# Gate r, value and hawk output as seven products of half matrices, with tokens on partitions, in a fused Hawk and RWKV block

## The chip, the cores and the metric

The kernel runs on one core of one Trainium2 chip. The metric is the device time of one execution in microseconds (us); the median of three runs of the kernel before is 644.53 us. The engines are TensorE (PE in the profile, its weight loads PEld), VectorE (DVE), ScalarE (ACT), GpSimd (POOL) and SyncE (SP), which here only issues DMAs.

## The reference

The input x has 8 sequences of 1024 tokens and 256 channels, all in fp32. The output is the sum of x and two branches that read the same normalized input.

```python
xn = _layernorm(x, axis=-1)
x = x + _L0_attn_ref(xn, ...) + _L0_ffn_ref(xn, ...)

# attn ("hawk"): 256 channels, 384 hidden
gate = einsum('bsd,hd->bsh', x, Wg)
u    = einsum('bsd,hd->bsh', x, Wi)
y    = conv1d(u, conv_w, 4 taps, causal, one per channel) + conv_b
ig   = sigmoid(einsum('bsh,gh->bsg', y, lru_Wi) + lru_bi)
rg   = sigmoid(einsum('bsh,gh->bsg', y, lru_Wg) + lru_bg)
alpha = exp(-8 * softplus(lam) * rg)
beta  = sqrt(1 - alpha**2 + 1e-6)
h     = scan over tokens: h[t] = alpha[t] * h[t-1] + beta*ig*y
out   = einsum('bsh,dh->bsd', gelu(gate) * h, Wo)

# ffn ("rwkv" channel mix): 256 channels
xr = mu_r * x + (1 - mu_r) * x_prev      # x_prev: x shifted by one token
xk = mu_k * x + (1 - mu_k) * x_prev
r  = sigmoid(einsum('btc,dc->btd', xr, W_r))
out = r * einsum('btc,dc->btd', square(relu(xk @ W_k.T)), W_v)
```

## The kernel before

The eight sequences are worked off one after the other. The input of a sequence is loaded with tokens on partitions (`xs`, two buffers), normalized there (`stats`, `deviation`, `inverse`, `normalize`), turned on TensorE by 16 transposes of 128 columns (`transposes`, L541) and kept with channels on partitions in `xnT`. From there come the branches:

- family u (gate and u, six blocks of 128 rows), family k (the key) and family l (the two lru gates, three chunks of 128 channels deep) run with channels on partitions: a weight block of 128x128 is loaded, and 512 tokens stream past it (`product`, L305). The output lies in one PSUM bank of 128x512.
- gate r (`r_product`), value (`v_product`) and the hawk output (`o_product`) run with tokens on partitions (`by_token`, L594): 128 tokens are the loaded operand, and the 256 columns of the weight stream past. r and value have two chunks of 128 channels, the hawk output three. A bank takes two tiles of 128 tokens.

Every fp32 matmul of the program appears in the trace as two passes, each with its own weight load.

**Seven products.** The families u, k and l do a 2x2 product of blocks (two row blocks, two channel chunks, two halves of 512 tokens) with seven products where eight would be needed, in the manner of Strassen and Winograd. The class `Group` holds one such set. Its token sums T0 to T3 are differences of halves of the input, made on GpSimd (`token_sum`, L302); its weight sums S0 to S3 are made once (`weight_sums`). Step 1 makes A and C, and ScalarE copies A into a new bank B (`seed`, L360) and C into SBUF (`five`, L365). Step 2 adds to A, which can then be evicted, and to B. Then VectorE's `fork_c` (L368) writes B + five into C, and step 3 adds to B (its first product) and to C. `fork_d` (L376) writes B + five to the place of the fourth quarter, and step 4 adds to B. A third chunk, as in family l, is added by plain products, and then the fourth quarter has a bank D and a step 5; without one, `late` finishes the fourth quarter from SBUF. An eviction of a quarter is `evict`; after it the bank is free.

**Order.** All instructions of all engines are put in one list of steps with a time, and the list is sorted. TensorE's products have times that follow one another (`pe`, `clock`, `now()`): one unit is one product of 512 columns, two passes. Everything else is put in by `at`, whose default time is relative to TensorE's clock and is replaced by an entry of the table `PLACES` where there is one (times in the same units from the start of the sequence; one table for the first, one for the middle, one for the last sequence). Each engine does its instructions in the order that comes out; semaphores see to the data. So a place fixes an order within an engine's queue, not a moment. In a middle sequence TensorE's order in before has 91 units: u, k, the end of the last sequence's l, then r, value, the hawk output of the sequence before (`outs`), the own l, and among that the transposes of the next sequence (`tp`).

**Around the change.** `add_x` (L629) adds x once more, by an accumulating DMA from GpSimd's queue into `sides` (two buffers, tokens on partitions), where r's tanh and then the value product are kept. `add_hawk` (L639) adds the hawk output to it on VectorE and issues the output's DMA on SP. `conv_rest` (L658) is the convolution's second to fourth tap, three each for three chunks; `mix` (L580) makes xk and xr; `recur` (L690) is the scan; `decay`, `decay_square`, `decay_rest`, `beta`, `gated_input`, `scaled_input`, `gated_state` surround it. `decay_rate` (L249 to L261) makes a constant of three columns. `key_home` is where the activated key lies: in `ysum`, in the last sequence in the first buffer of x.

Of the kernel before, what the change touches and what calls it, by code (L numbers as in the profile page):

```python
# [10 lines left out]
ALU = mybir.AluOpType  # L11
# [23 lines left out]
        "u0_0 evict 0 0": 2.36, "u0_0 evict 1 0": 3.48, "u0_0 evict 0 1": 6.36, "u1 seed": 9.36,  # L35
        "u0_0 evict 1 1": 10.05, "u1 five": 10.73, "stats 0 8": 10.89, "u2 seed": 11.41,
        "conv_first 1": 12.09, "u1 evict A 0 0": 13.51, "u2 five": 14.19, "k seed": 15.36,
        "u1 fork_c": 16.16, "stats 0 1": 16.96, "k five": 17.27, "stats 1 1": 17.69,
        "conv_first 0": 17.95, "u2 fork_c": 18.36, "deviation": 19.3, "u1 fork_d": 19.36,
        "u2 evict A 0 0": 21.18, "inverse 0 8": 21.66, "u1 evict C 0 1": 21.86, "k fork_c": 22.36,  # L40
        "k evict A 0 0": 22.54, "conv_first 2": 23.22, "u2 fork_d": 23.36, "conv_rest 0 1": 24.17,
        "u2 evict C 0 1": 24.57, "normalize 0 1": 25.25, "stats 2 1": 25.66, "u1 evict B 1 0": 25.95,
        "k fork_d": 26.36, "normalize 1 1": 26.64, "conv_rest 0 2": 27.17, "k late": 27.34,
        "normalize 2 1": 28.02, "conv_rest 1 1": 28.66, "u2 evict B 1 0": 28.73, "k evict B 1 0": 29.41,
        "conv_rest 0 3": 30.16, "k evict C 0 1": 31.19, "conv_rest 2 1": 31.65, "r_tanh 0": 32.97,
        "conv_rest 1 2": 33.13, "r_tanh 2": 33.66, "normalize 3 1": 34.34, "conv_rest 2 2": 34.63,
        "normalize 4 1": 35.03, "r_tanh 4": 35.74, "conv_rest 1 3": 36.12, "normalize 5 1": 36.42,
        "normalize 6 1": 37.11, "conv_rest 2 3": 37.61, "r_tanh 6": 37.81, "normalize 7 1": 38.5,
        "stats 3 1": 39.09, "u1 late": 39.19, "value 0": 39.75, "u2 late": 39.87, "stats 4 1": 40.55,
        "y_sum 0": 40.86, "stats 5 1": 41.27, "value 2": 41.93, "y_sum 1": 42.09, "stats 6 1": 42.73,  # L50
        "value 4": 43.38, "stats 7 1": 44.19, "y_sum 2": 44.86, "value 6": 45.36, "y_sum 3": 46.02,
        "l0 seed": 46.3, "add_x": 46.98, "l0 five": 47.15, "l0 evict A 0 0": 49.36, "l0 fork_c": 50.36,
        "l1 seed": 51.36, "put_transposed 0 0": 52.86, "put_transposed 1 0": 53.44, "l1 five": 54.01,
        "put_transposed 0 1": 54.69, "l0 fork_d": 55.36, "put_transposed 1 1": 55.38, "x_sum 0": 55.54,
        "mix_before k 0": 56.06, "x_sum 2": 56.7, "mix_before k 1": 57.29, "mix k 0": 57.87,
        "l0 evict C 0 1": 58.51, "mix_before r 0": 59.31, "mix k 1": 59.36, "l0 evict B 1 0": 60.54,
        "mix r 0": 60.86, "l1 evict A 0 0": 61.36, "mix_before r 1": 62.16, "x_sum 1": 62.36,
        "l1 fork_c": 62.36, "l0 evict D 1 1": 63.39, "k_sum 0": 63.52, "l2 seed": 64.36,
        "mix r 1": 64.68, "l2 five": 65.36, "decay 0": 66.05, "k_sum 1": 66.18, "l1 fork_d": 66.36,
        "x_sum 3": 67.35, "decay 1": 67.39, "k_sum 2": 68.51, "l1 evict C 0 1": 68.73,  # L60
        "decay_square 0": 69.53, "k_sum 3": 69.67, "l2 evict A 0 0": 70.64, "l2 fork_c": 71.36,
        "decay 2": 71.44, "decay_rest 0": 72.17, "decay_square 1": 72.78, "l1 evict B 1 0": 73.89,
        "decay_rest 1": 74.06, "l1 evict D 1 1": 74.69, "l2 fork_d": 75.36, "decay_square 2": 75.49,
        "decay_rest 2": 77.59, "l2 evict C 0 1": 86.13
    },
    "middle": {
        "gated_input 0": -0.83, "beta 0": 0.33, "stats 0 1": 0.59, "stats 1 1": 1.32, "u0 seed": 1.56,
        "scaled_input 0": 1.98, "beta 1": 2.24, "stats 2 1": 3.4, "u0 five": 3.47, "recur 0 L": 4.06,
        "beta 2": 4.15, "u0 evict A 0 0": 5.38, "stats 3 1": 5.52, "recur 0 R": 6.18,
        "l2 evict B 1 0": 7.56, "u0 fork_c": 7.63, "gated_state 0": 8.44, "l2 evict D 1 1": 9.16,  # L70
        "gated_input 1": 9.86, "u1 seed": 9.96, "k seed": 10.64, "gated_input 2": 11.29,
        "u1 five": 11.32, "k five": 12.01, "u0 fork_d": 12.71, "scaled_input 1": 13.52,
        "deviation": 14.19, "u0 evict C 0 1": 14.57, "scaled_input 2": 14.94, "u1 evict A 0 0": 15.25,
        "conv_first 0": 15.93, "u1 fork_c": 16.37, "recur 1 L": 17.17, "k evict A 0 0": 17.28,
        "u0 evict B 1 0": 18.36, "k fork_c": 18.63, "conv_first 1": 19.12, "recur 2 L": 19.43,
        "u2 seed": 20.46, "recur 1 R": 20.89, "u2 five": 21.14, "u1 fork_d": 22.34,
        "u1 evict C 0 1": 22.36, "conv_first 2": 23.12, "recur 2 R": 23.14, "k fork_d": 24.6,
# [70 lines left out]
def kernel(  # L148
# [182 lines left out]
    class Group:  # L331
# [11 lines left out]
        def step(self, n):  # L343
# [34 lines left out]
            def late():  # L378
                self.out(1, 1, "sbuf")
# [673 lines left out]
```

## Time and profile before

| what | us |
|---|---|
| median of 3 runs | 644.53 (644.47 to 645.62) |
| the profiled execution, its own time | 645.16 |
| its span in the profile | 643.2 |
| TensorE busy in the span | 637.7 (99%) |
| VectorE / ScalarE / GpSimd busy | 469.5 / 458.9 / 186.4 |
| the same in a middle sequence, 314.90 to 393.25 (78.35) | 57.74 / 57.41 / 20.82 |

The granted clock of TensorE was 1.0 in the profiled execution. The durations of matmuls in the profile are from the start of a pass to its modelled end, and passes overlap; so the spacing of starts, which the chain gives as a stretch's length for so many passes, says what a pass costs TensorE. In the rows of groups the columns are line, engine, operation, output and inputs with their shape, count, busy time in us, mean ns of one, and the idle time before. The table of stretches has the stretch and its length, then busy us and count for PE, PEld, DVE, ACT and POOL, the granted clock, the DMA share and GB/s.

### The profile page before, as it was taken

The page shows a single profiled execution, that of the slowest core. Times are in us where ns is not written, and L with a number is a line of the kernel's source. Part 1 is how long each engine was busy: PE and PEld are TensorE (multiplying, and loading weights), DVE is VectorE, ACT ScalarE, POOL GpSimd, SP SyncE. Part 2 cuts the span into 40 slices and gives each one's busy share as a digit, 9 for nine tenths or more (in the row PEclk, how much of TensorE's full clock was granted, in tenths as well). Part 3 has the DMA queues.
Part 4 walks back from the last instruction along what each step waited for, and adds up shares of the span by engine and source line. Part 5 has one row for each costly group of instructions (what it writes and reads, how often), then busy time and mean ns, then how long its engine had stood idle before and what let it go on. Part 6 is the DMA issues. An engine that isn't in the chain of part 4 may idle for free.

```text
span 643.2 us, 5932 instructions
## 1 busy us (share of the span) xinstructions
PE 637.7 (99%) x2032; PEld 372.6 (58%) x2032; DVE 469.5 (73%) x602; ACT 458.9 (71%) x646; POOL 186.4 (29%) x131
## 2 busy tenths in 40 slices
PE   9999999999999999999999999999999999999997
PEld 4475446864468544775447754486544865456466
DVE  4896799656995669847699377992779827798395
ACT  3895998368873888639885398845988269883870
POOL 4926600443004620047101380022800328104000
PEclk9999999999999999999999999999999999999999
DMA  9205100260004400052000520006000060000412
GB/s 317 77 1 92 40 0 1 41 155 2 0 1 67 130 0 1 1 102 94 0 0 2 114 83 0 0 1 114 18 0 0 2 114 17 1 0 1 65 34 98
DMA packets 27549, 28.70 MB, mean 45 GB/s; under 512 B 1152, under 2 KB 27008, under 8 KB 27520
## 3 DMA queue, kind: packets, MB, share of 16 engines
q1 hardware_dynamic: 18784, 19.53, 9.4%
q0 software_dynamic: 8320, 8.39, 8.7%
q10 hardware_dynamic: 416, 0.41, 0.2%
q8 instruction: 16, 0.26, 0.2%
q14 instruction: 13, 0.11, 0.1%
HBM read 19.94 MB, written 8.39 MB: 44 GB/s over the span
## 4 chain that ended last, share of the span: by engine, by line
PE 98%; DVE 1%; ACT 0%; issue 0%; DVEq 0%
PE bank L305 65%; PE bank L594 30%; PE bank L541 2%; PE bank L776 1%; DVE st L514 0%; ACT x L536 0%; ACT u L445 0%; DVE xnT L558 0%; ACT xnT L560 0%; DVE mv L516 0%; DVE side L639 0%; DVE mv L527 0%; DVEq L1048 0%; ACT std L519 0%; DVE five L752 0%
## 5 line engine op out<-in xcount | busy, mean ns | idle before, releaser
L305 PE MATMUL bank<-y,w_l 128*128 128x512 f32 x288 | 137.8, 592 | 0.0
L302 POOL TENSOR_TENSOR ysum<-y 128x512 f32<-128x512 f32 x16 | 24.2, 1513 | 298.1 <-PE bank L594 277.6
L305 PEld LDWEIGHTS bank<-y,w_l 128*128 128x128 f32 x288 | 54.6, 190 | 62.6 <-issue 61.2
L658 DVE SCALAR_TENSOR_TENSOR y<-u,par,y 128x1024 f32<-128x1024 f32 x72 | 88.8, 1288 | 0.0
L594 PE MATMUL bank<-w_o,g 128*128 128x256 f32 x384 | 86.1, 379 | 0.0
L594 PEld LDWEIGHTS bank<-w_o,g 128*128 128x128 f32 x384 | 73.0, 190 | 15.9 <-issue 6.7
L305 PE MATMUL bank<-ysum,sum_l 128*128 128x512 f32 x144 | 72.3, 593 | 0.0
L305 PE MATMUL bank<-xsum,sum_u 128*128 128x512 f32 x138 | 69.1, 592 | 0.0
L536 ACT ACTIVATE x<-x,mv,std 128x256 f32<-128x256 f32 x60 | 31.6, 591 | 52.0 <-DVE mv L527 52.0
L368 DVE TENSOR_TENSOR bank<-bank,five 128x512 f32<-128x512 f32 x55 | 38.0, 691 | 38.5 <-PE bank L305 38.5
L594 PE MATMUL bank<-w_r,xr 128*128 128x256 f32 x256 | 58.8, 379 | 0.0
L594 PEld LDWEIGHTS bank<-w_r,xr 128*128 128x128 f32 x256 | 48.6, 190 | 16.0 <-issue 8.9
L457 ACT ACTIVATE tr<-bank,half_b 128x512 f32<-128x512 f32 x48 | 32.3, 687 | 31.5 <-PE bank L305 31.5
L305 PE MATMUL bank<-xnT,w_u 128*128 128x512 f32 x108 | 54.1, 593 | 0.7 <-ACT xnT L560 0.7
L639 DVE TENSOR_TENSOR side<-side,bank 128x512 f32<-128x512 f32 (+1 forms) x36 | 22.1, 624 | 41.8 <-PE bank L594 41.8
L376 DVE TENSOR_TENSOR bank<-bank,five 128x512 f32<-128x512 f32 x24 | 16.8, 699 | 44.8 <-PE bank L305 44.8
L594 PE MATMUL bank<-w_v,ysum 128*128 128x256 f32 x224 | 49.5, 379 | 0.0
L360 ACT COPY bank<-bank 128x512 f32<-128x512 f32 x55 | 31.7, 577 | 22.9 <-PE bank L305 22.2
L594 PEld LDWEIGHTS bank<-w_v,ysum 128*128 128x128 f32 x224 | 42.6, 190 | 5.8
L302 POOL TENSOR_TENSOR xsum<-xnT 128x512 f32<-128x512 f32 x16 | 21.1, 1331 | 84.4 <-ACT xnT L560 84.4
L305 PEld LDWEIGHTS bank<-ysum,sum_l 128*128 128x128 f32 x144 | 26.7, 190 | 31.0 <-issue 26.5
L305 PEld LDWEIGHTS bank<-xsum,sum_u 128*128 128x128 f32 x138 | 26.1, 189 | 30.1 <-issue 28.3
(113 smaller groups left out, 1147.4 us busy)
## 6 DMA issues: line engine op xcount, KB each, us to landing
side<-in_x_dram POOLq DMA_DIRECT2D x8, 1024.0 KB, 11.0
x<-in_x_dram SPq DMA_DIRECT2D x7, 1024.0 KB, 5.5
out_dram<-side SPq DMA_DIRECT2D x28, 256.0 KB, 3.6
x<-in_x_dram SPq DMA_DIRECT2D x4, 256.0 KB, 4.3
out_dram<-side SPq DMA_DIRECT2D x8, 128.0 KB, 1.7
w_l<-in_lru_wg_dram SPq DMA_DIRECT2D x1, 576.0 KB, 6.0
w_l<-in_lru_wi_dram SPq DMA_DIRECT2D x1, 576.0 KB, 7.0
w_u<-in_w_i_dram ACTq DMA_DIRECT2D x1, 384.0 KB, 3.9
```

Of the source, the lines that this page charges most:

```text
L302: nc.gpsimd.tensor_tensor(dst[o], a, b, ALU.subtract)
L305: nc.tensor.matmul(banks[b], lhsT, rhs, start=start, stop=True, skip_group_check=True)
L360: nc.scalar.copy(banks[bank["B"]], banks[bank["A"]])
L368: nc.vector.tensor_tensor(banks[bank["C"]], banks[bank["B"]], self.five, ALU.add)
L376: nc.vector.tensor_tensor(d, banks[bank["B"]], self.five, ALU.add)
L457: nc.scalar.activation(dst[:, m, HALVES[h]], src, AF.Tanh, bias=half_b[:, b + m : b + m + 1], scale=0.5)
L536: nc.scalar.activation(xa, xa, AF.Identity, bias=m, scale=r)
L541: nc.tensor.matmul(banks[b][:, t * P : (t + 1) * P], xs[s % 2][:, 4 * h + t, c * P : (c + 1) * P], ident, is_transpose=True, start=(t == 0 ...
L594: nc.tensor.matmul(banks[b][:, j * D : (j + 1) * D], lhs[:, c, (t + j) * P : (t + j + 1) * P], weights[w][:, c, :], start=(j == 0 and c == 0),
L639: nc.vector.tensor_tensor(o, o, two_tiles(b)[:, j : j + n, :], ALU.add)
L658: nc.vector.scalar_tensor_tensor(y[:, m, :], u[:, m, k : k + S], column(COL_CONV_W + k * HC + m), y[:, m, :], ALU.mult, ALU.add,)
L776: nc.tensor.matmul(banks[b], warm[:, 0:P], warm, start=True, stop=True)
```

## The change

Gate r, value and the hawk output become `Group`s of seven products too, with tokens on partitions. A product of such a group takes a half of 512 tokens, one chunk of channels and 128 of the 256 output columns, and runs as four matmuls, one for each tile of 128 tokens, each with 128 columns of weight (`product_by_token`). A quarter of the result lies in a bank as four tiles of 128 tokens by 128 columns and goes to a quadrant of `sides`. r is a group in all sequences, value in all but the first, the hawk output (with a third chunk in plain products) for all sequences but the last two; those keep `by_token`. In a middle sequence TensorE's list has 88 units instead of 91.

The token sums of the new groups need room: `sums_for` gives r three buffers of its own and half of xr, value those of x (`xsum`), k the buffer in `sides` of the same sequence, the hawk output `tr`. x has one buffer `xt` instead of two; sequence s + 2 is loaded after the transposes of s + 1, at time `now() + 1`, and all its statistics are in the places from 73 on. The constants of `decay_rate` are steps of their own and have early places, and the places of everything are new. In the table of the last sequence `add_hawk` has no entries any more.

TensorE's order in a middle sequence after, from unit 28, with the length of each step: r 1 (2), u2 3 (2), r 2 (2), u2 4 (1), r 3 (2), v 1 (2), r 4 (1), v 2 (2), o 1 (2), v 3 (2), o 2 (3), v 4 (1), o 3 (3), l0 1 (2), o 4 (2), l0 2 (3), o 5 (1), l1 1 (2), transposes (2, to unit 65), l0 3 (3), l0 4 (2), l1 2 (3), l0 5 (1), l2 1 (2), l1 3 (3, from 76), and the rest to 88.

```diff
+        "early weight_sums u": 0.0, "early constant 0": 1.04, "early constant 1": 1.44,
+        "u0_0 evict 0 0": 2.36, "u0_0 evict 1 0": 3.49, "early weight_sums k": 3.93,
...
+        "gated_state 2": 29.24, "r seed": 30.54, "token_sum o 1": 30.66, "r five": 31.22,
+        "u2 fork_d": 31.36, "token_sum o 2": 31.82, "k evict C 0 1": 31.9, "inverse 0 8": 32.97,
+        "token_sum o 3": 33.34, "u2 evict C 0 1": 33.69, "r evict A 0 0": 34.27, "r fork_c": 34.27,
+        "token_sum v 0": 34.38, "normalize 0 1": 34.79, "conv_rest 0 1": 35.33, "u2 evict B 1 0": 35.42,
+        "normalize 1 1": 36.1, "normalize 2 1": 36.8, "r fork_d": 36.82, "token_sum v 1": 36.82,
+        "r evict C 0 1": 37.49, "conv_rest 0 2": 37.97, "v seed": 38.36, "normalize 3 1": 39.04,
+        "token_sum v 2": 39.46, "v five": 39.74, "r evict B 1 0": 40.42, "conv_rest 0 3": 40.61,
+        "normalize 4 1": 41.09, "normalize 5 1": 41.79, "token_sum v 3": 42.09, "v fork_c": 42.36,
+        "normalize 6 1": 42.49, "v evict A 0 0": 43.16, "normalize 7 1": 43.18, "token_sum y 0": 43.25,
+        "o seed": 43.88, "conv_rest 1 1": 44.4, "o five": 44.56, "r late": 45.24, "v fork_d": 45.89,
+        "u2 late": 45.92, "conv_rest 2 1": 46.69, "v evict C 0 1": 48.17, "o fork_c": 49.36,
+        "conv_rest 1 2": 49.93, "conv_rest 2 2": 51.33, "o fork_d": 52.81, "conv_rest 1 3": 53.61,
+        "l0 seed": 54.36, "conv_rest 2 3": 55.11, "l0 five": 55.36, "o evict A 0 0": 56.6,
+        "token_sum y 1": 56.6, "token_sum y 2": 57.75, "o evict C 0 1": 58.2, "token_sum y 3": 58.92,
+        "v evict B 1 0": 59.0, "l0 evict A 0 0": 59.36, "v late": 60.08, "l0 fork_c": 60.88,
+        "add_x": 61.04, "l1 seed": 62.36, "put_transposed 0 0": 63.86, "put_transposed 1 0": 64.44,
...
+        "mix k 1": 71.53, "l0 evict B 1 0": 71.54, "l1 evict A 0 0": 72.36, "stats 0 1": 73.02,
+        "token_sum k 0": 73.02, "mix_before r 1": 73.16, "l1 fork_c": 73.75, "token_sum x 3": 74.19,
+        "l0 evict D 1 1": 74.39, "stats 1 1": 74.56, "decay 0": 75.19, "mix r 0": 75.35,
+        "l2 seed": 76.53, "stats 2 1": 76.85, "token_sum k 1": 76.85, "l2 five": 77.21,
+        "l1 fork_d": 77.58, "decay_square 0": 77.9, "token_sum k 2": 78.01, "stats 3 1": 78.38,
...
+        "own l2 fork_d": 76.36, "own scaled_input 1": 77.17, "own recur 1": 79.39,
+        "own l2 evict C 0 1": 79.86, "own l2 evict B 1 0": 80.66, "own decay 2": 81.46,
+        "own gated_input 2 L": 82.09, "own l2 evict D 1 1": 82.8, "own gated_state 1 L": 82.9,
+        "own decay_square 2": 83.6, "own recur 0 R": 83.69, "own decay_rest 2": 85.14,
+        "own gated_input 2 R": 85.95, "own gated_state 0 R": 86.74, "own gated_state 1 R": 87.54,
+        "own beta 2": 87.59, "own scaled_input 2 L": 88.98, "own recur 2 L": 89.91,
+        "own gated_state 2 L": 91.5, "own scaled_input 2 R": 91.92, "own recur 2 R": 92.78,
+        "own gated_state 2 R": 94.37
     },
...
-    xs = [fixed(f"x{n}", [TT, D]) for n in range(2)]
+    xt = fixed("xt", [TT, D])
...
+    r_parts = [fixed(f"rsum{n}", [NT]) for n in range(3)]
+
+    def sums_for(which, s):
+        if which == "r":
+            own = list(r_parts)
+        else:
+            home = {"x": xsum, "y": ysum, "v": xsum, "k": sides[s % 2], "o": tr}[which]
+            home = home if which in "xyv" else home.rearrange("p a b -> p (a b)")
+            own = [home[:, i, :] if which in "xyv" else home[:, i * NT : (i + 1) * NT] for i in range(4)]
+        if which in "kr":
+            own = [own[0], mixes[which][:, 0, HALVES[1]], own[1], own[2]]
+        return own
...
+        yield lambda: scalar(e, lam, AF.Abs)
+        yield lambda: scalar(e, e, AF.Exp, scale=-1.0)
...
+    def product_by_token(b, weight, tokens, start=False):
+
+        for j in range(4):
+            p = slice(j * P, (j + 1) * P)
+            nc.tensor.matmul(
+                banks[b][:, p],
+                tokens[:, p],
+                weight,
+                start=start and j == 0,
+                stop=True,
+                skip_group_check=True,
+            )
...
+    def r_group(s):
+        def place(r, h, src, spare=None):
+            dst = quadrant(s, r, h)
+            if src is not None:
+                nc.scalar.activation(dst, src, AF.Tanh, scale=0.5)
+            return dst
+
+        return Group("r", "r", 0, (0, 1), halves_for("r", s), sums_for("r", s), place, by_token=True)
+
+    def v_group(s):
+        def place(r, h, src, spare=None):
+
+            if src is None:
+                return spare
+            o = quadrant(s, r, h)
+            nc.vector.scalar_tensor_tensor(o, o, 1.0, src, ALU.add, ALU.mult)
+
+        return Group("v", "v", 0, (0, 1), halves_for("v", s), sums_for("v", s), place, by_token=True)
...
+            nc.vector.tensor_tensor(o, o, src, ALU.add)
+            done[h] += 1
+            if done[h] == 2:
+                nc.sync.dma_start(out_rows(s, 4 * h, 4), sides[s % 2][:, 4 * h : 4 * h + 4, :])
+
+        half = halves_for("o", s)
+        return Group(
+            "o", "o", 0, (0, 1), half, sums_for("o", s), place, third=lambda h: half(2, h), by_token=True
+        )
...
-        load(1, 0, TT)
...
+        at(4.5, load, 1, 0, TT)
+        token_sums(4.05, 0, "x")
         mixing(4.2, 5.5, "k")
-        for i in range(4):
-            at(9 + i / 10, k_sum, i)
-        mixing(12.2, 18.2, "r")
+        token_sums(9, 0, "k")
+        mixing(10, 12, "r")
+        token_sums(16, 0, "r")
         at(8, halve, "v")
         at(1.5, weight_sums, "k")
+        at(13, weight_sums, "r")
         at(30.0, weight_sums, "l")
-        rate = None
-
-        def constants():
-            nonlocal rate
-            rate = decay_rate()
-
-        at(45.7, constants)
+        at(40, weight_sums, "v")
+        at(41, weight_sums, "o")
...
                 ks.step(4)
-                gates(s, 0)
-                gates(s, 2)
+                rs.step(3)
+                rs.step(4)
...
+                rs.step(1)
                 us[2].step(3)
-                gates(s, 2)
+                rs.step(2)
                 us[2].step(4)
+                rs.step(3)
...
+            elif not last:
+                token_sums(b + 36.5, s, "v")
+                vs.step(1)
+                rs.step(4)
+                vs.step(2)
+                token_sums(b + 41.5, s - 1, "o")
+                os.step(1)
+                vs.step(3)
+                os.step(2)
+                vs.step(4)
+                at(now() + 1, add_x, s)
+                token_sums(now() + 1.1, s, "y")
+                os.step(3)
+                ls[0].step(1)
+                os.step(4)
+                ls[0].step(2)
+                os.step(5)
+                ls[1].step(1)
...
-                    if first:
-                        at(b + 10, load, s + 2, 0, TT)
-                    if s + 3 < B:
-                        at(now() + 1, load, s + 3, 0, TT)
+                    at(now() + 1, load, s + 2, 0, TT)
                     for t in range(TT):
                         at(now() + 11.3 + t, stats, s + 2, t, 1)
-                for i in range(4):
-                    at(now() + 1.5 + i / 10, x_sum, i)
+                token_sums(now() + 1.5, s + 1, "x")
...
+                token_sums(b + 36.5, s, "v")
+                vs.step(1)
+                rs.step(4)
+                vs.step(2)
                 at(b + 8, weight_sums, "l", True)
-                for i in range(4):
-                    at(now() - 1 + i / 10, y_sum, i)
+                token_sums(now(), s, "y")
                 ls[0].step(1)
-                values(s, 4)
+                vs.step(3)
                 ls[0].step(2)
+                vs.step(4)
+                at(now() + 1, add_x, s)
...
-                outs(s - 1, 0, add=d + 15.2)
+                outs(s - 1, 0)
```

## Prediction

> **What bounds the kernel now.** I read the first block of the page, what TensorE waited for, the chain that ended last, timelines of single stretches, and then the groups of VectorE and GpSimd.
>
> ```profile
> PE 637.7 (99%) x2032; PEld 372.6 (58%) x2032; DVE 469.5 (73%) x602; ACT 458.9 (71%) x646; POOL 186.4 (29%) x131
> ```
>
> TensorE is busy from end to end. The list of its waits has two entries, both in the first 17 us:
>
> ```profile
> PE bank L776 <- DVE five L752: 1.2, 1, 1.2
> PE bank L305 <- ACT xnT L560: 0.7, 1, 0.7
> ```
>
> The chain is TensorE's own stream (start, length, passes):
>
> ```profile
> 345.13 15.54 PE bank L594 x72
> 369.26 1.82 PE bank L541 x16
> 376.25 41.20 PE bank L305 x96
> ```
>
> So every pass that goes is worth its spacing in that stream, as long as no new wait opens. The spacing, not the mean duration of a record, is the price: 15.54 us / 72 = 0.2158 us for a pass of 256 columns (its record is 0.379) and 41.20 / 96 = 0.429 us for one of 512. A middle sequence repeats every 78.35 us (345.13 to 423.48 in the chain).
>
> **What a pass of 128 columns costs.** The only such passes now are the transposes:
>
> ```profile
> 369.10 1.47 PE L541 MATMUL bank<-ident,x 128*128 128x128 f32 x12
> 369.10 1.98 PE L541 MATMUL bank<-ident,x 128*128 128x128 f32 x16
> 370.81 0.30 PEld L305 LDWEIGHTS bank<-ysum,sum_l 128*128 128x128 f32 x2
> 370.92 1.02 PE L305 MATMUL bank<-ysum,sum_l 128*128 128x512 f32 x2
> ```
>
> The first row cuts the window after 12 passes, the second has all 16. Without the last record's 0.272 us, 12 passes take (1.47 - 0.27) / 11 = 0.109 us each. All 16 give 1.82 / 16 = 0.114 in the chain, because one break of about 0.08 lies among them. A transpose's weight load takes 0.141 us and an ordinary fp32 load 0.190, so the doubt is whether ordinary loads keep up. The third row answers: two ordinary loads within 0.30 us begin 0.11 apart, and the matmul of the first begins at 370.92, 0.11 after the load began at 370.81. So I take 0.109 and count breaks apart. The far end is 0.190, a load that has to end first; I give it little, since that row shows the contrary.
>
> The rule that speaks against this stands in the Trainium skill, "TensorE: Matmul & The Clock Gate", section "The mechanism": a weight load overlaps a running matmul only when it goes to other rows of the array. By it a pass here would be 0.190 + 0.109 = 0.30 us and the kernel would end near 890 us; the 72 passes above, each with a 0.190 load, at 0.2158 spacing contradict it.
>
> **Part by part, TensorE.** r had 16 products of 256 columns, 32 passes: 32 x 0.2158 = 6.91 us a sequence. It becomes seven products of four tiles, 56 passes: 56 x 0.109 = 6.10. That is 0.81 saved, and value is the same. The hawk output had 48 passes, 10.36 us; seven products and four for the third chunk are 88 passes, 9.59 us: 0.77 saved. r changes in all 8 sequences, value in 7 (the first keeps the old form), the output in 6 (those of the last two keep it). 15 x 0.81 + 6 x 0.77 = **16.8 us** off. With 0.114 instead, it is 10.
>
> Breaks: each of the 21 groups has about one product that waits for two engines; at 0.08 each that is **1.6 us** back (0 to 5, if every product had one).
>
> **New waits inside a group.** Step 3 may start only when VectorE's fork_c, after step 2, has read bank B. Wherever two or more other products lie between, before has no wait. The change leaves one product, 0.86 to 0.87 us, between the steps in these places: r's steps 2 and 3 in every sequence (us[2].step(4) or ks.step(4)), r's fork_d in the first, and the output's steps 2 and 3 in six. What such a turn takes is seen once in before:
>
> ```profile
> 68.51 2.06 PE L305 MATMUL bank<-ysum,sum_l 128*128 128x512 f32 x4
> 68.71 0.69 DVE L368 TENSOR_TENSOR bank<-bank,five 128x512 f32<-128x512 f32 x1
> 69.45 0.30 PEld L305 LDWEIGHTS bank<-ysum,sum_l 128*128 128x128 f32 x2 [0.74 <-DVE bank L368]
> ```
>
> From the fork's start to the load is 0.74, and 0.11 more to the matmul. Ahead of it the last pass of 128 needs its record, 0.27, and about 0.04 to 0.11 to wake VectorE. From the start of that pass: 0.27 + 0.07 + 0.74 + 0.11 = 1.19. TensorE has work for 0.11 + 0.86 = 0.97. So 0.2 us is lost, 0.23 with some lateness; 8 + 1 + 6 = 15 places: **3.5 us**.
>
> **VectorE, ScalarE, GpSimd.** Each group adds two forks (0.69 each), a seed and a five copy (0.58) and four token sums. A middle sequence gets 4.1 us on VectorE (57.7 of 78.35 now), 3.5 us on ScalarE (57.4 now) and 12 x 1.27 = 15 us on GpSimd (20.8). Evictions stay four for each product. All three fit beside 76 us of TensorE; the exclusion between two of them is the doubt:
>
> ```profile
> L658 DVE SCALAR_TENSOR_TENSOR y<-u,par,y 128x1024 f32<-128x1024 f32 x72 | 88.8, 1288 | 0.0
> L580 DVE SCALAR_TENSOR_TENSOR xk<-xnT,par,xk 128x1024 f32<-128x1024 f32 x16 | 32.4, 2064 | 5.7 <-ACT xk L574 5.7
> L302 POOL TENSOR_TENSOR xsum<-xnT,xsum 128x512 f32<-128x512 f32 x16 | 32.2, 2010 | 0.1
> L302 POOL TENSOR_TENSOR ysum<-y,ysum 128x512 f32<-128x512 f32 x16 | 22.2, 1388 | 7.3 <-DVE y L658 6.8
> ```
>
> The same form takes 1.29 us in the convolution, which meets few sums, and 2.06 in the mixing, which meets one each time: a meeting costs VectorE 0.78, and the sum grows from 1.27 to 2.01. Reads from PSUM (L368) stay at 0.69 throughout. From r's third step to the output's last, 26 products or 22.5 us, VectorE now has 9 convolutions, six forks and about six evictions: 9 x 1.29 + 12 x 0.69 = 19.9 us, beside eight sums (value's, y's). The places put v 1 and v 2 between convolutions, v 3 and y 0 under v's fork, and y 1 to 3 behind the last convolution: I count three meetings, 2.3 us, and 22.2 fits in 22.5. I take **0** here; with all eight, 26.1, it misses by 3.6.
>
> The Trainium skill, "SBUF — State Buffer", section "Who interferes with whom", says the loser of this pair blocks for the other's whole instruction. By that a meeting would be 1.27 instead of 0.78, three would make 23.7 and the stretch would miss by 1.2 us a sequence, some 7 us in six.
>
> **Start.** The decay constants move from 45.7 to the front: Abs and Exp now stand on ScalarE between the second normalize (L536) and the u evictions (L445), and these are on the chain:
>
> ```profile
> 14.02 1.09 ACT x L536 x2
> 15.12 0.95 ACT u L445 x2
> 16.07 0.50 ACT xnT L560
> L250 ACT ACT_TABLE_LOAD x1 | 1.3, 1283 | 0.0
> ```
>
> The table load comes with Exp: 0.19 + 1.28 + 0.21 = **1.7 us** later for xnT, which TensorE and the x sums wait for. Nothing covers it. The r, v and o weight sums, 4 x 0.46 each, queue on GpSimd among the x, k and r sums; walking its queue at 1.3 to 2.1 us a sum, each lands before its product. The load of x 1 moves behind the first transposes on SP; its 5.5 us end before its statistics.
>
> **The one buffer for x.** Each load must now follow the transposes on SP, and the statistics follow at once (place 73.0, load 66). On VectorE l1's fork_c is queued behind the first statistics, and l1's third step on TensorE waits for that. Meanwhile add_x, which waits for v's late quadrant and on GpSimd for the y sums, moves from place 49 to 61:
>
> ```profile
> side<-in_x_dram POOLq DMA_DIRECT2D x8, 1024.0 KB, 11.0
> x<-in_x_dram SPq DMA_DIRECT2D x7, 1024.0 KB, 5.5
> 363.00:365.00 2.00, 2.00 (x11) 1.77 (x10) 0.00 (x0) 0.12 (x1) 0.00 (x0) 1.00 1.21 222
> ```
>
> The last figure of the third row is GB/s with add_x and output DMAs together; the load alone moves 350 (373 to 375). In before add_x (357.58) is done when the load goes out (371.15). Walking the queues, add_x now goes out 53.0 us into a sequence, the output's second half at 54.5 and the load at 56.9. At its first packet, 1.45 later, some 0.6 MB of add_x and 0.27 of the output are left. add_x takes half of 222, 5.3 us; 0.8 MB remain at 350, 2.2; with 0.6 to land that is 9.5 us. The load ends at 66.4, statistics (0.55), fork (0.69) and restart (0.16) at 67.8, and the product's time is 66.3: 1.5 us lost. At 296 GB/s, the best slice of that overlap, 0.4. I take the middle, 0.8, since little output is left when the load starts. Six loads: **4.8 us** (0 to 9).
>
> **End.** The last sequence's add_hawk pieces have no places any more and fall into VectorE's queue between gated_state, scaled_input and recur of the last third, in front of the output's third chunk: two or three of 0.69, partly under ScalarE's beta. I count **1.0 us** (0 to 2).
>
> **Sum.** 16.8 - 1.6 - 3.5 - 1.7 - 4.8 - 1.0 = 4.2 off. The profiled execution took 645.16 (span 643.2, 2.0 around it), so 641.0; it lies 0.6 above the median 644.53, hence **about 640.4**.
>
> **Rivals.** (1) Slower: VectorE becomes the bound in the stretch above. It decides once more than three of the eight sums meet a convolution: then v's and the output's forks come late and TensorE waits for each. With all eight, 3.6 us x 6 = 22 on top: 662; with five, 1.3 x 6, 648. For it: VectorE is busy 14.07 of 15.00 us in the stretch before (330 to 345), and GpSimd's queue cannot choose its moment. Against it: the places alternate sums and convolutions, and records of VectorE's neighbours overlap by 0.09 us, some 2 us in all. (2) The load of x lands as late as the even sharing says: 6 x 1.5 = 9 for 4.8, 644.6, and to 650 where the work queued behind the statistics piles up too. (3) The load is not late, and forks and breaks half hidden: 645.2 - 16.8 + 2.6 + 1.7 + 1.0 - 0.6 = 633. (4) Ordinary weight loads don't keep up: 0.190 a pass adds 15 x 3.7 + 6 x 6.4 = 94, some 745. That the change doesn't do what it says is none here: the passes are counted from its loops.
>
> **How the numbers follow.** Forecast (637 to 643.2) 0.36; (3), 629 to 637, 0.22; (2), 643.2 to 650, 0.22; (1), 646 to 664, 0.17; (4) 0.03. A measurement here tells 0.2%, 1.3 us, from no change, so of (2) 0.10 counts as the same. Faster 0.36 + 0.22 = 0.58; same 0.10; slower 0.12 + 0.17 + 0.03 = 0.32. The range 631 to 652 leaves out the upper half of (1), (4) and the edge of (3); the forecast's own is 637 to 643.2.
>
> **What would show it.** Right: passes of 128 columns 0.109 apart; a middle sequence of about 77.5 us; waits of TensorE of 0.2 us for the fork at r and the output, and of about 0.8 at l1's third step, behind statistics that wait for the load; the first long stretch of TensorE starting near 18.3 us. Wrong: spacing near 0.19; convolutions with a mean far over 1.4 us and TensorE waiting 1 us or more for v's and the output's forks (1); a load landing in 6 us (3); a sequence over 78.4 us.

## The result, and the profile after

The kernel after takes 653.62 us (median of 4 runs, 652.42 to 655.85), the kernel before beside it 645.02: a ratio of 1.0137, 95% interval 1.0106 to 1.0168. It is slower by 1.4%, and lies 1.6 us above the upper end of the range. Its profiled execution took 654.12 us, with a span of 652.2 (before 645.16 and 643.2).

The engines, from the first block of the page:

```profile
PE 632.6 (97%) x2632; PEld 379.8 (58%) x2632; DVE 503.0 (77%) x644; ACT 484.7 (74%) x691; POOL 315.7 (48%) x227
```

TensorE is busy 5.1 us less than before, in a span that is 9.0 us longer. So it stands still more than before, and the list of its waits says where (who waited, for whom: us in total, times, longest):

```profile
PE bank L340 <- DVE bank L425: 11.4, 6, 2.5
PE bank L340 <- ACT xnT L651: 2.3, 1, 2.3
PE bank L859 <- DVE five L836: 1.2, 1, 1.2
```

The first entry is new: six waits, one for each sequence that loads the x of two sequences on, for `fork_c` (L425). The chain of waits of one of them, in order (start, us, what):

```profile
352.23 16.55 PE bank L346 x144
...
379.32 10.58 DMA xt<-in_x_dram
...
389.92 0.44 DVE st L605
...
390.39 0.18 DVE mv L607
390.57 0.60 DVE bank L425
...
391.21 8.83 PE bank L340 x16
```

The load of x goes out at 379.32 and lands 10.58 us later. The first statistics start 0.02 us after that, l1's `fork_c` stands behind them in VectorE's queue, and TensorE's third step of l1 waits for the fork. The issues of DMAs give the landing times (KB each, median us from issue to landing); before, the load took 5.5:

```profile
side<-in_x_dram POOLq DMA_DIRECT2D x8, 1024.0 KB, 11.2
xt<-in_x_dram SPq DMA_DIRECT2D x7, 1024.0 KB, 9.9
```

What follows such a wait is not in any list of waits. In the table of stretches (stretch and length; busy us and count of PE, PEld, DVE, ACT, POOL; granted clock; DMA share; GB/s), before the wait and after it:

```profile
380.00:388.00 8.00, 8.00 (x20) 3.56 (x19) 4.86 (x3) 7.45 (x11) 7.91 (x6) 1.00 1.17 252
392.65:394.30 1.65, 1.65 (x3) 0.66 (x2) 1.61 (x5) 0.69 (x1) 1.27 (x1) 0.50 0.00 0
```

The clock is 0.50 just after it: four passes of 512 columns start 0.853 us apart instead of 0.429, and 1.7 us are lost that no engine is to blame for. It happens behind two of the six waits of this execution. The four executions have granted clocks of 0.997, 0.997, 0.994 and 0.991 and took 652.42, 653.12, 654.12 and 655.85 us, so how often it happens is not the same in each.

### The profile page after: what moved, and what is told of

It reads as the page before. It is cut to its first block, busy times and chain, and to the rows that moved or that the text cites. A ratio compares the mean times of both kernels' runs of the same rounds, so it can differ in the third digit from the quotient of the medians.

```text
span 652.2 us, 7422 instructions
## 1 busy us (share of the span) xinstructions
PE 632.6 (97%) x2632; PEld 379.8 (58%) x2632; DVE 503.0 (77%) x644; ACT 484.7 (74%) x691; POOL 315.7 (48%) x227
## 4 chain that ended last, share of the span: by engine, by line
PE 71%; DMA 10%; POOL 7%; DVE 5%; issue 4%; ACT 1%; SPq 0%; DVEq 0%; POOLq 0%
PE bank L340 48%; PE bank L346 20%; DMA xt<-in_x_dram 9%; PE bank L690 3%; POOL xsum L663 2%; DVE y L746 1%; DVE bank L425 1%; POOL tr L663 1%; DVE g L782 1%; ACT xnT L651 1%; DMA w_u<-in_w_g_dram 1%; PE bank L632 1%; POOL rsum L663 1%; POOL side L663 1%; DVE st L605 0%
## 5 line engine op out<-in xcount | busy, mean ns | idle before, releaser
L425 DVE TENSOR_TENSOR bank<-bank,five 128x512 f32<-128x512 f32 x76 | 52.8, 694 | 46.2 <-PE bank L346 17.0
L663 POOL TENSOR_TENSOR ysum<-y,ysum 128x512 f32<-128x512 f32 x16 | 28.4, 1775 | 64.0 <-DVE y L746 64.0
L422 ACT COPY five<-bank 128x512 f32<-128x512 f32 x76 | 44.4, 586 | 6.5 <-PE bank L340 4.2
L663 POOL TENSOR_TENSOR tr<-g,tr 128x512 f32<-128x512 f32 x12 | 20.2, 1679 | 58.2 <-DVE g L782 58.2
L605 DVE BATCH_NORM_STATS2 st<-xt 128x6 f32<-128x256 f32 x64 | 25.4, 411 | 27.6 <-DMA xt<-in_x_dram 27.6
L433 DVE TENSOR_TENSOR bank<-bank,five 128x512 f32<-128x512 f32 x30 | 20.7, 692 | 28.4 <-PE bank L340 20.3
L346 PE MATMUL bank<-w_o,g 128*128 128x128 f32 x288 | 37.0, 275 | 0.0
L346 PEld LDWEIGHTS bank<-w_o,g 128*128 128x128 f32 x288 | 35.0, 192 | 2.9 <-issue 2.9
L514 ACT ACTIVATE ti<-bank,half_b 128x512 f32<-128x512 f32 x48 | 32.2, 686 | 5.9 <-PE bank L340 5.4
L340 PEld LDWEIGHTS bank<-xnT,w_u 128*128 128x128 f32 x108 | 20.4, 190 | 27.6 <-issue 22.5
L680 DVE SCALAR_TENSOR_TENSOR xk<-xnT,par,xk 128x1024 f32<-128x1024 f32 x16 | 31.2, 1982 | 5.2 <-ACT xk L674 5.2
## 6 DMA issues: line engine op xcount, KB each, us to landing
side<-in_x_dram POOLq DMA_DIRECT2D x8, 1024.0 KB, 11.2
```

Source lines behind the costliest of these rows:

```text
L340: nc.tensor.matmul(banks[b], weight, tokens, start=start, stop=True, skip_group_check=True)
L346: nc.tensor.matmul(banks[b][:, p], tokens[:, p], weight, start=start and j == 0, stop=True, skip_group_check=True,)
L422: nc.scalar.copy(self.five, banks[bank["C"]])
L425: nc.vector.tensor_tensor(banks[bank["C"]], banks[bank["B"]], self.five, ALU.add)
L433: nc.vector.tensor_tensor(self.d, self.view(banks[bank["B"]]), self.view(self.five), ALU.add)
L514: nc.scalar.activation(dst[:, m, HALVES[h]], src, AF.Tanh, bias=half_b[:, b + m : b + m + 1], scale=0.5)
```

## The experiments

Each ratio is to the kernel before on the same chip. All start from the kernel after; all but those of number 9 only move entries of the order, so the work is the same.

**1. add_x behind the load.**

```diff
-"add_x": 50.18 (first)   "add_x": 61.04 (middle)
+"add_x": 66.0            "add_x": 76.0
```

> Only the place of add_x moves: from 50.18 to 66.0 in the first sequence, from 61.04 to 76.0 in the middle ones, behind the load of x instead of just ahead of it. Theory A (the load of x shares the DMA engines with add_x, lands 9.9 us after its issue, the first statistics hold VectorE's queue, l1's fork_c stands behind them, TensorE idles 1.6 to 2.7 us six times, 12.4 us, and the two longest idles are followed by four passes at half the clock, 3.4 us): the load lands in about 5.5 to 6.5 us, the three long entries of TensorE's waits (11.4, 2.3 and 1.2 us together now) shrink to under 3, the granted clock goes back to 1.0, the time falls by 13 to 16 us to 637 to 641 us. Rival B (VectorE is overloaded by the sums and convolutions, and the wait at l1 only shows it): the load lands sooner, but the fork comes late all the same; under 4 us gained, 650 us or more. Rival C (a load of x into one buffer is slow for another reason, its wait for the transposes): it still takes about 9 us.

Measured: 648.28 us, ratio 1.0044 (1.0028 to 1.0059); 5.3 us less than the change. Issues of DMAs and TensorE's waits:

```profile
xt<-in_x_dram SPq DMA_DIRECT2D x7, 1024.0 KB, 5.2
```

```profile
PE bank L340 <- DVE bank L425: 5.0, 6, 1.1
PE bank L340 <- ACT xnT L651: 2.3, 1, 2.3
PE bank L340 <- DVE bank L433: 1.5, 5, 0.3
```

Rival C falls: with add_x out of the way the load lands in 5.2 us, in the same single buffer. No wait is left at l1. But only a third of the gain is there, and the waits are other ones: l2's `fork_c` (L425) and `fork_d` (L433). VectorE's groups and its timeline and GpSimd's around one of them say why:

```profile
L680 DVE SCALAR_TENSOR_TENSOR xr<-xnT,par,xr 128x1024 f32<-128x1024 f32 x16 | 47.8, 2990 | 0.0
```

```profile
385.82 1.55 POOL L717 DMA_DIRECT2D side<-in_x_dram  x1
386.77 1.91 POOL L663 TENSOR_TENSOR side<-xk,side 128x512 f32<-128x512 f32 x1
388.05 1.85 POOL L663 TENSOR_TENSOR xk<-xk 128x512 f32<-128x512 f32 x1
...
388.80 4.64 DVE L680 SCALAR_TENSOR_TENSOR xr<-xnT,par,xr 128x1024 f32<-128x1024 f32 x1
389.28 1.85 POOL L663 TENSOR_TENSOR side<-xk,side 128x512 f32<-128x512 f32 x1
390.51 1.83 POOL L663 TENSOR_TENSOR rsum<-xr 128x512 f32<-128x512 f32 x1
...
394.44 0.68 DVE L425 TENSOR_TENSOR bank<-bank,five 128x512 f32<-128x512 f32 x1
```

In the kernel after, the same group is:

```profile
L680 DVE SCALAR_TENSOR_TENSOR xr<-xnT,par,xr 128x1024 f32<-128x1024 f32 x16 | 23.9, 1495 | 0.0
```

In run 1 add_x's issue took GpSimd 1.55 us and let token sums pile up; they then ran without a gap, 1.23 us apart, and a single mixing of VectorE that began among them lasted 4.64 us. So the exclusion of rival (1) of the prediction is real, but it decided in another place and for another reason. That reading was argued only; run 3 tests it. add_x's transfer, which also runs beside this mixing, is not enough by itself: in the kernel after, two mixings in a row (from 381.56) took 4.16 us together while add_x and the load were both under way.

**2. The statistics behind l1's forks,** with add_x and the load as in the change.

```diff
-"stats 0 1": 73.02, "stats 1 1": 74.56, "stats 2 1": 76.85, "stats 3 1": 78.38, ...
+"stats 0 1": 79.3, "stats 1 1": 79.4, "stats 2 1": 80.67, "stats 3 1": 80.75, ...
```

> add_x and the load stay as in the change; the statistics of x move in VectorE's queue from 60 to 78 (first sequence) and 73 to 81 (middle) to behind l1's forks (66.9 on, and 79.3 on). Theory A: the load still takes 9 to 10 us, but no fork of l1 stands behind statistics that wait for it; TensorE's wait at l1's third step (11.4 us in six) falls under 2 and the clock stays at 1.0; the time falls by 12 to 16 us to 638 to 642 us. A normalize that comes later could cost up to 1 us a sequence at the next transposes. Rival B (VectorE overloaded, or TensorE slowed by the DMA traffic itself): under 4 us gained, 650 us or more.

Measured: 642.39 us, ratio 0.9962 (0.9949 to 0.9975): 11.2 us less than the change, and faster than before. TensorE's waits:

```profile
PE bank L340 <- ACT xnT L651: 2.3, 1, 2.3
PE bank L340 <- DVE bank L433: 2.0, 4, 0.5
```

The load still took 9.8 us, and nobody on the path minded. So it is not the transfer that costs, but the queue that it holds up. What is missing to the 16 us of the waits at l1 and the half clock behind them is at l2's forks: in four middle sequences the fourth step of l2 came 0.66 us late, behind the statistics that now lie there, with 0.1 for each restart, and its third step some 0.2 late.

**3. add_x in GpSimd's gap.**

```diff
-"add_x": 50.18 (first)   "add_x": 61.04 (middle)
+"add_x": 83.5            "add_x": 95.0
```

> add_x moves once more, from behind the load of x (66.0 and 76.0, the run before) to the stretch in which GpSimd has nothing to do, behind r's token sums of the next sequence (83.5 and 95.0). In the run before, the load landed in 5.2 us and still only 5.3 us of 16 were gained. Theory A2: what ate the rest is add_x's issue on GpSimd (1.55 us), which bunched three token sums together; they held VectorE's mixing (xr, 4.64 us for one, mean 2.99 against 1.50), and l2's forks stood behind it (waits of 5.0 + 1.5 us). With add_x in the gap: xr's mean back near 1.5 to 1.7, these two waits under 1.5 together, 637 to 641 us, that is 7 to 11 less than with add_x at 76. Rival B2: VectorE is simply full ahead of l2's forks once the statistics come in time; xr may get shorter, but the forks stay late and the time is 645 to 649 us.

Measured: 638.41 us, ratio 0.9895 (0.988 to 0.991); about 10 less than run 1. Groups of VectorE, and all of TensorE's waits:

```profile
L680 DVE SCALAR_TENSOR_TENSOR xr<-xnT,par,xr 128x1024 f32<-128x1024 f32 x16 | 26.7, 1667 | 0.0
```

```profile
PE bank L340 <- ACT xnT L651: 2.2, 1, 2.2
PE bank L859 <- DVE five L836: 1.2, 1, 1.2
```

A2 holds: the mixing is back at 1.67 us, the waits at l2 are gone, and the statistics, which come as early as in run 1, disturb nothing. Runs 1 to 3 together show the price of the one buffer as it was placed: 653.6 - 638.4, some 15 us. In the profiled execution of run 3 the half clock once follows the wait at the start.

**4. Two products between the steps of r and of the output.**

```diff
                 rs.step(2)
                 us[2].step(4)
-                rs.step(3)
...
                 vs.step(1)
-                rs.step(4)
+                rs.step(3)
                 vs.step(2)
+                rs.step(4)
...
-                os.step(3)
                 ls[0].step(1)
+                os.step(3)
                 os.step(4)
```

> TensorE's order is changed so that two products instead of one lie between the steps of r (second and third, third and fourth; seven sequences) and of the output (second and third; six): r 3 goes behind v 1, r 4 behind v 2, and o 3 behind l0's first step, with fork_d and the evictions behind it moved along. If the forks' turn is longer than the one product that covers it: 7 x 0.33 + 6 x 0.24 = 3.7 us less, about 650 us, and the waits of 0.2 us in front of these steps gone from the chain. If those 0.2 us are the groups' ordinary breaks, or come back behind v's forks: no change within 1 us.

Measured: 650.32 us, ratio 1.0088 (1.0055 to 1.012), 3.3 less than the change. In its chain of waits the stretch that begins with r's late steps has no fork in front and no break inside:

```profile
352.44 0.86 PE bank L340 x2
353.31 13.40 PE bank L346 x120
```

13.40 / 120 is 0.1117 us a pass; the change has 16.55 / 144 = 0.1149 there, with the output's waits in it, and 0.25 us for r's fork ahead of it. So the waits inside the groups are the ones predicted, at about their price (3.7 was expected). The half clock blurs this comparison; between executions of the same granted clock, 0.997, the gain is 3.9: 648.36 and 649.40 against 652.42 and 653.12.

**5. The constants back at one place,** and **6. the start freed.**

```diff
 run 5: all "early constant" entries of the first table removed (default 45.7)
 run 6:
-"early constant 0": 1.04, "early constant 1": 1.44, "early constant 2": 3.98, ...
-"early weight_sums r": 3.99, "early weight_sums o": 4.0
+"early constant 0": 16.75, "early constant 1": 16.76, "early constant 2": 28.3, ...
+"early weight_sums r": 15.4, "early weight_sums o": 30.5
```

> The decay constants lose their early places and go back to the one place 45.7 in the first sequence, as in the kernel before. If the table load for Exp ahead of the u evictions on ScalarE delays the first xnT half: 1.6 us less, 652.0 us; the second stretch of TensorE starts near 16.6 instead of 17.7 us. If the start was bound elsewhere (GpSimd's weight sums): no change within 0.5 us.

> Only the start: the constants' Abs and Exp go behind the second use of Sqrt on ScalarE (from 1.04 and 1.44 to 16.75), the three VectorE constants behind them follow (28.3), and GpSimd's weight sums for r and the output go behind the k sums (15.4, 30.5) and no longer stand ahead of the x sums. In the run with the constants at 45.7 TensorE's first wait fell from 2.46 to 0.81 us, but a new one of 0.68 for the x sum opened behind it, and the constants' chain on VectorE then held the convolution for 6.7 us. Theory: both terms of the start gone, 1.5 to 1.8 us less, 651.9 us, with no wait for a convolution. Rival: Exp's table load only moves, and costs the same in front of gelu's: under 0.5 us gained.

Measured: run 5 (whose line numbers lie 7 lower) 658.51 us, ratio 1.0214 (1.0191 to 1.0236); run 6 653.51, 1.0129 (1.0112 to 1.0146), no different from the change. TensorE's waits, of run 5 and then of run 6:

```profile
PE bank L333 <- DVE y L739: 6.5, 1, 6.5
...
PE bank L333 <- ACT xnT L644: 0.6, 1, 0.6
```

```profile
PE bank L340 <- DVE y L746: 1.2, 1, 1.2
...
PE bank L340 <- ACT xnT L651: 0.7, 1, 0.7
```

Both misses. The table load does delay the first transposed half: without it that wait is 0.6 to 0.7 instead of 2.3 us. But the 1.6 us won come back as a wait for the first sequence's convolution (y): 1.2 us in run 6, and 6.5 in run 5, where all the constants stood right ahead of its last tap. With the late start of the change there is no such wait: the start's loss hides it, as far as these runs show.

**7. The remedies together:** run 2's statistics (three of the eight behind l2's last fork), run 4's order, run 6's start.

> The three remedies in one: the statistics behind l1's forks (here the last three of them behind l2's last fork too, 86.5), two products between the steps of r and of the output, and the start of the run above. If the three causes are separate, their gains add: 653.6 - 11.2 - 3.3 - 1.6 and 3 more for l2's step 4, which waited 0.66 us four times in the run with the statistics late, gives 634.5 to 638 us, 1.0 to 1.6% less than the kernel before. If they share a cause (VectorE full everywhere), the sum falls short: 640 us or more.

Measured: 633.86 us, ratio 0.9822 (0.9806 to 0.9839): 1.8% faster than the kernel before and the best of all. All waits of TensorE that are left:

```profile
PE bank L340 <- DVE y L746: 1.2, 1, 1.2
PE bank L859 <- DVE five L836: 1.2, 1, 1.2
PE bank L340 <- ACT xnT L651: 0.7, 1, 0.7
```

That is just under the 634.5 to 638 expected of separate causes, and far from the 640 of a shared one. By themselves runs 2, 4 and 6 gained 11.2, 3.3 and 0.1, which is 14.6; together they gain 19.8. The trace accounts for it: the 16.4 us of the load's waits and the half clock behind them are gone whole, since the statistics of run 2 no longer hold l2 up either, some 3.5 are gone at r's and the output's steps, and the start gives next to nothing, as in run 6.

**8. add_x in the gap, run 4's order, the start, and the constants' VectorE work behind the convolution** (50.5 on).

> add_x in GpSimd's gap (83.5, 95.0; 638.4 us by itself), two products between the steps of r and of the output, the weight sums for r and the output behind the k sums, Abs and Exp behind the second Sqrt, and all the constants' VectorE work behind the first sequence's convolution (50.5 on), since the start's gain came back as a wait of 1.4 us for that convolution when they stood at 28.3. Theory, from the ledger of the run with add_x in the gap (start 2.5, half clock behind it 1.7, r's and the output's steps 4.4, other breaks 1): 638.4 - 3.7 - 1.6 - 1.7 = 631.4; if the half clock at the start is not to be had or the convolution's wait stays, 633 to 634. If the convolution's wait grows with nothing of VectorE's to take away, 635.

Measured: 634.84 us, ratio 0.9839 (0.9825 to 0.9854), where 631.4 was expected, or 633 to 635 if the convolution's wait stayed. TensorE's waits:

```profile
PE bank L340 <- DVE y L746: 1.2, 1, 1.2
PE bank L859 <- DVE five L836: 1.2, 1, 1.2
PE bank L340 <- DVE bank L433: 1.0, 1, 1.0
PE bank L340 <- ACT xnT L651: 0.7, 1, 0.7
```

The half clock at the start is gone, but the wait for the convolution stays at 1.2 us though no constant is ahead of it, and the constants, moved, hold up a fork of l0 for 1.0. What else holds the first convolution was not settled.

**9. What a group is worth by itself.** Value of the six middle sequences goes back to four plain products of 256 columns, in run 3's kernel. A first version had the first eviction ahead of r's eviction of B, so that part of r was written over the value and the output is wrong:

> The kernel with add_x in GpSimd's gap (638.4 us), in which the value product of the six middle sequences goes back to four plain products of 256 columns (32 passes instead of 56); r, the output and the last sequence keep the seven products. It tells what a group is worth where nothing else stands in the way. By passes: 32 x 0.2158 = 6.91 against 56 x 0.1116 = 6.25 us, 0.66 a sequence, so 4.0 us more: 642 to 643 us. If the group's forks, seeds and sums had cost the path as much as its passes save (VectorE or GpSimd at their limit): 638 us or less. VectorE falls by 12 forks (8 us) less what the evictions differ, GpSimd by 24 token sums (some 35 us).

It took 641.20 us, ratio 0.9945 (0.9928 to 0.9963), and is not counted. The second has it behind:

```diff
-                vs.step(1)
+                values(s, 0)
                 rs.step(4)
-                vs.step(2)
+                values(s, 2)
...
-                vs.step(3)
+                values(s, 4)
                 os.step(2)
-                vs.step(4)
+                values(s, 6, 1)
```

> Value of the six middle sequences as four plain products of 256 columns in the kernel with add_x in GpSimd's gap (638.4 us), as in the run before, with the first of their evictions behind r's eviction of B (41.0 instead of 39.1), so that r's tanh lies under it. Theory: a value group saves 6.91 - 56 x 0.1116 = 0.66 us of passes a sequence, and the output's forks, which wait 0.24 us a sequence with the group's short fourth step between them, lose that wait here: +0.42 us a sequence, 2.5 us in six, 640.9 us; a sequence of 77.45 instead of 77.03 us. Rival: the group's forks, seeds and sums hold up the path beside that: 638.4 us or less.

Measured: 640.07 us, ratio 0.993 (0.9916 to 0.9943), against 0.9895 for run 3: the group is worth 0.35%, 2.3 us in six sequences. In the chains a middle sequence takes 77.45 us (343.60 to 421.05) against 77.03 in run 3 (343.40 to 420.43), which is the 0.42 expected. The chain of this run has both kinds of pass side by side (L690: 256 columns, L346: 128):

```profile
345.62 1.73 PE bank L690 x8
347.35 0.89 PE bank L346 x8
...
353.49 2.68 PE bank L346 x24
```

1.73 / 8 = 0.216 and 2.68 / 24 = 0.1117 us, each with its weight load: the saving of the passes is there, and the group's forks, seeds and token sums cost the path nothing once no queue holds them up, beside the 0.24 a sequence that the output's forks wait.

## Why the prediction was wrong

The sign was wrong: 4.2 us off were forecast, 9.0 were added. The measured side of the ledger comes from the trace of the kernel after (the execution of 654.12 us), as the time between the starts of neighbouring passes beyond 0.109, 0.216 and 0.429 us, less the same in before:

| term of the sum | predicted | measured |
|---|---|---|
| passes saved, at 0.109 | -16.8 | -16.8, but +3.5 since a pass is 0.1116 |
| breaks and waits inside the groups | +1.6, +3.5 | +4.4 |
| start | +1.7 | +1.6 |
| the one buffer: TensorE's waits | +4.8 | +13.0 |
| the one buffer: half clock behind them | - | +3.4 |
| end | +1.0 | +0.1 |
| sum | -4.2 | +9.2 (spans differ by 9.0) |

**The step that failed** is "I take the middle, 0.8, since little output is left when the load starts". The mechanism was right to the queue: load, statistics, `fork_c`, l1's third step, and the order of issue too (add_x 3.7 us ahead of the load; 3.9 were worked out). The even sharing with add_x gave a landing in 9.5 us and 1.5 us lost; 9.9 was measured, and the six waits are 2.17, 1.98, 1.63, 1.87, 2.68 and 2.06, mean 2.07, with 0.1 more for each restart: 13.0 in all for the 4.8 of the sum. The middle was taken between this and a row at 296 GB/s that was an overlap of other transfers (and the middle of 0.4 and 1.5 is 0.95, not 0.8). The prediction had the better number in hand and averaged it away; with 1.5 its sum would have been 644.6, with 2.17 a sequence 648.6. Of the 0.57 us between 1.5 and 2.07, 0.4 is the later landing; the rest is open.

**The term that was missing** is the clock. Nothing in the profile of before could price it: its granted clock was 1.0. In the traces of all twelve kernels, ten of the sixteen idles of TensorE of 2.1 us and more were followed by half rate, nearly all for four passes of 512, 1.6 to 1.8 us; of those in the loop up to 2.06 us none was. The Trainium skill ("TensorE: Matmul & The Clock Gate", section "Why this matters for your kernels") advises against idle gaps over about 3 us; here 2.17 us was enough. Its section "What's actually happening" has the window in which activity is judged run freely, which would make the outcome a matter of where an idle falls in it.

The traces agree. In their record of the granted clock, every change in the program lies on a grid of 3.413 us: in the kernel after the clock is 0.50 for 3.41 us from 74.25 and from 391.69, and the 314.03 at full clock between them are 92 such steps. Two steps of that grid, each with the one behind it (columns as in the table of stretches above):

```profile
388.28:391.69 3.41, 0.89 (x2) 0.30 (x2) 1.70 (x6) 3.40 (x5) 3.29 (x3) 1.00 0.03 9
391.69:395.10 3.41, 3.41 (x5) 1.33 (x4) 3.34 (x8) 1.65 (x2) 1.27 (x1) 0.50 0.00 0
470.20:473.61 3.41, 1.51 (x5) 0.79 (x5) 2.73 (x6) 3.40 (x5) 2.89 (x3) 1.00 0.00 1
473.61:477.02 3.41, 3.41 (x10) 1.50 (x9) 3.34 (x8) 3.19 (x5) 1.27 (x1) 1.00 0.00 0
```

In the twelve traces all ten steps at full clock in which TensorE was busy for 1.44 us or less were followed by half clock, and none in which it was busy for 1.51 or more. So an idle of 2.17 us that lies almost whole in one step (1.44 busy) was followed by half clock, and one of 2.71 that two steps share (run 5, 2.34 and 1.93 busy) was not. Which of the six waits is met is luck: the grid does not start with the program, and the first change that the record shows comes 3.84 to 6.95 us into the span, differently in each trace.

**A pass of 128** costs 0.1116 in a long stretch, not the 0.109 of the 12 transposes: 2.6 ns over 1346 passes is 3.5 us. That is midway to the 0.114 that the prediction named as the other price, and a little nearer to it.

**The waits inside the groups** came where predicted: 0.33 us a sequence at r, 0.24 at the output (0.23 predicted for each). With 0.29 at r's fourth step in the first sequence these make the whole 4.4, so the 1.6 of separate breaks did not show. (The upper end given for those, 5 if every product had one, does not come out either: 171 products at 0.08 are 13.7.) **The start** was right in size, but run 6 shows that undoing it gains 0.1: the convolution's wait takes the 1.6 back. **The end** cost 0.1; the pieces of add_hawk held up next to nothing.

**The rivals.** (2) happened, and beyond its upper end of 650: without the 3.4 of the half clock the execution of 654.12 would have taken 650.7. (1) did not: v's and the output's forks make no wait behind a convolution, though its mean rose:

```profile
L746 DVE SCALAR_TENSOR_TENSOR y<-u,par,y 128x1024 f32<-128x1024 f32 x72 | 100.1, 1415 | 0.2
```

That is 0.127 more for each of 72, 9 us in all, or one and a half meetings a sequence at 0.78 (three were counted). (3) is what run 3 shows: 638.4 without the load's delay. At 633 it lay too low by the 3.5 of the passes and by taking forks and breaks as half hidden (2.6, measured 4.4); what the half clock at the start adds is not shown, since run 3's two executions with a granted clock of 0.996 took no more than 0.3 us longer than the two with 0.999. (4) is refuted by the 0.1117 (and its own sum comes to 751, not 745).

## What to carry to other kernels

When a second buffer is given up, write down which instruction first waits for the refill and what stands behind it in that engine's queue: the statistics were not needed before the next sequence's deviation, and moving them (run 2) gained 11 us with the transfer as slow as ever. Where two transfers are certain to overlap, take the even sharing, not a mean with a better case. A wait of 2 us on TensorE may cost 1.7 us more behind it, by where it falls on the clock's grid, so many short waits are cheaper than one long one of the same sum, as long as they are spread out.

## What the hardware showed that was not expected

- One VectorE instruction with two operands in SBUF lasted 4.64 us (1.27 alone) while three queued token sums of GpSimd ran past it 1.23 us apart: the queue of sums held it for the whole queue, not for one sum. The prediction's 0.78 for a meeting is the price of a single one. The Trainium skill ("SBUF — State Buffer", section "Who interferes with whom") says that the one who issues first takes the shared port for a whole instruction; that the other can lose several times in a row is what run 1 adds.
- The accumulating DMA of 1 MB took 9.2 us with no load beside it (run 1) and 11.2 with one, the plain load of 1 MB 5.2 and 9.9. Here the plain one, which started 3.7 us later, lost more (4.7) than the accumulating one (2.0).
- The half rate behind idles of TensorE of 2.17 us and more, and the grid of 3.413 us that decides which of them, told above.
